# Two early input quads loaded in pairs, and one division moved ahead of a normalization, in a transformer block on one NeuronCore

## The chip, the cores and the metric

The kernel runs on one core of a Trainium2 chip. The metric is device time in microseconds. Three runs of the kernel before took 2637.81 us in the median (2637.12 to 2638.28).

## What is computed

The input x has the shape (2, 256, 128, 128): batch, time, frequency band, channel. Three residual steps follow each other:

```python
xt = _ln(x, ln_t_w, ln_t_b).transpose(0, 2, 1, 3)
x = x + _mha(xt, t_wi, t_bi, t_wo, t_bo, 4, cm).transpose(0, 2, 1, 3)   # causal, over the 256 times
xf = _ln(x, ln_f_w, ln_f_b)
x = x + _mha(xf, f_wi, f_bi, f_wo, f_bo, 4, bm)                         # |i-j| <= 16, over the 128 bands
xn = _ln(x, ln_n_w, ln_n_b)
h = jax.nn.gelu(xn @ w1.T + b1, approximate=False)
x = x + (h @ w2.T + b2)
```

`_ln` is a layer normalization over the 128 channels, `_mha` an attention with 4 heads of 32 channels. All is float32.

## The kernel before, in words

The work is cut into groups of 512 tokens, four tiles of 128. First come all groups of the attention over time (class `OverTime`): 64 per batch, each with two bands at all 256 times. After them come the groups over the bands (`OverBands`) and of the two-layer network (`FeedForward`), in runs of 32 times. The change touches only the first groups over time. They are called by their number here: group 0 to group 3 share one quad of input, `k.x0`; groups 4 to 7 share the second quad, groups 8 to 11 the third, groups 12 to 15 the fourth. A quad is a tile of 128 partitions by 16 by 128 floats, 1 MB, and it is filled by four DMAs of 256 KB, each of which fills 32 partitions. So any group of a quad needs all four of them.

Nothing is reordered by a planner here. Every operation goes through the helper `InOrder` (line 904 of the profile, for that reason) and keeps the order in which the Python code emits it, on its own engine. `start` (line 1197) emits the head, and `run` (line 1261) then runs a loop over n. In the round n of that loop the engines do, interleaved: the second half of the scores of group n and the first half of those of group n+1 on TensorE (`time_scores`, line 754); the exponentials on ScalarE; the masks and a sum on GpSimd; the output product of group n-2 (`output`, `finish`) and the sums and products with the values of group n-1 (`weigh`); the reciprocal by two functions of ScalarE and the division on VectorE for group n-1 (`invert`, `divide`, lines 602 and 615); and the queries, keys and values of group n+2 (`queries_keys`, `values`).

A group's path to TensorE has these steps. `load` (line 382) issues its part of the quad on SyncE's queue. `statistics` (line 390) is four BATCH_NORM_STATS2 and four BATCH_NORM_AGGREGATE on VectorE. Then the inverse root, by GpSimd (`root`) or for several groups together by ScalarE with a refinement on VectorE (`Four`, `root_in_bank`, `refine`, line 429). `normalize` (line 441) is four TENSOR_SCALAR on VectorE into `xh`; `turn` (line 458) is a 32x32 block transpose on VectorE into `z` and four DMAs into a DRAM tile, `turned`; `fetch` (line 470) is one DMA from it into `xnT`. SyncE's queue issues all of these DMAs in their order in the program, and an issue that has to wait holds up all behind it. The first four groups are transposed by TensorE instead (`turn_by_tensor`, line 483), and then copied from PSUM by VectorE.

`divide` works on the PSUM banks of the sums and the weighted values: a product into the bank, `u`, then `oT`. These two banks are taken again by the scores of the next round, so TensorE's scores wait for `u` and `oT`.

The head also loads weights: `rows` (three bias rows, each broadcast to 128 partitions), `w1T` (256 KB) and others. `add_rows` (line 1110) needs the first two rows and `fold_hidden` (line 1180) needs `w1T`, both in round 0. In the kernel before, round 0 emits the four loads of the third quad early in its text and two of the fourth quad's later, round 1 the other two; a round's place in the program is no time, and SyncE issues them as soon as its queue comes to them.

Of the kernel before, what the change touches and what calls it, by code (L numbers as in the profile page):

```python
# [25 lines left out]
NT = 4  # L26
# [7 lines left out]
HALF = P // 2  # L34
# [8 lines left out]
def load_constants(ctx, tc, x, t_wiT, t_woT, f_wiT, f_woT, w1T, w2T, cols, rows):  # L43
    nc = tc.nc
    B, T, FB, C = x.shape
    k = Consts()
    k.NI = w1T.shape[1] // P
    const = ctx.enter_context(tc.tile_pool(name="const", bufs=1))
    k.const = const
    sync, scalar = InOrder(tc, nc.sync), InOrder(tc, nc.scalar)  # L50
    k.x0 = const.tile([P, NT, NT, C], F32, name="x0")

    def tokens(g, n, queues):
        for i in range(NT):
            f = i // (T // P) * NT + g
            queues[i % 2].dma_start(k.x0[rows_of(i), :, g : g + n], BoundedPath.of_times(x[0], i, slice(f, f + n)))

    def weight(src, n, name, queue=sync):
        t = const.tile([P, n], F32, name=name)
        queue.dma_start(t, src)  # L60
        return t

    def rows_in(a, b):
        for i in range(a, b):
            sync.dma_start(k.rows[:, i, :], rows[i : i + 1, :].partition_broadcast(P).squeeze(1))

    def late_weights():
        k.w2T = const.tile([P, k.NI, C], F32, name="w2T_sb")
        sync.dma_start(k.w2T, w2T.rearrange("(j p) c -> p j c", p=P))

    tokens(0, 1, (sync, scalar))
    k.cols = const.tile([P, 16], F32, name="cols_sb")
    sync.dma_start(k.cols, cols)
    k.wiT = [weight(t_wiT, 3 * C, "t_wiT_sb", scalar)]
    scalar.preload_act_table_set(EXP_SET)
    tokens(1, 1, (sync, sync))
    tokens(2, 2, (sync, sync))
    k.woT = [weight(t_woT, C, "t_woT_sb")]
    k.rows = const.tile([P, 3, C], F32, name="rows_sb")
    rows_in(0, 2)  # L80
    k.wiT.append(weight(f_wiT, 3 * C, "f_wiT_sb"))
    k.woT.append(weight(f_woT, C, "f_woT_sb"))
    k.load_w1T = lambda: setattr(k, "w1T", weight(w1T, k.NI * P, "w1T_sb"))
    k.late_weights, k.late_rows = late_weights, lambda: rows_in(2, 3)
    k.ones = const.tile([P, P], F32, name="ones")
    nc.vector.memset(k.ones, 1.0)
    k.ident = const.tile([P, P], F32, name="ident")
    make_identity(nc, k.ident)
    k.mhalf = const.tile([P, NT], F32, name="mhalf")
    nc.vector.memset(k.mhalf, -0.5)  # L90
    dram = ctx.enter_context(tc.tile_pool(name="dram", bufs=1, space=DRAM))
    k.x1 = [dram.tile([T, FB, C], F32, name=f"x1_{b}") for b in range(B)]
    return k
# [548 lines left out]
def rows_of(h):  # L642
    return slice(h * D, (h + 1) * D)
# [265 lines left out]
class BoundedPath:  # L909
# [71 lines left out]
    def groups(self, x, out):  # L981
        nc, k = self.nc, self.k
        B, T, FB, C = x.shape
        NC_T = T // P
        for b in range(B):
            for f0 in range(0, FB, GA):
                held = {}


                def load(g, f0=f0, b=b, held=held):  # L990
                    if b == f0 == 0:
                        held["x"] = k.x0
                        return
                    if g == 0:
                        self.input_quad(held)
                        if b == 0 and f0 == 2 * NT:
                            self.vector.memset(held["x"][:, 0, 0, 0:1], 0.0)
                    f = f0 + g // NC_T * NT
                    self.sync.dma_start(held["x"][rows_of(g)], self.of_times(x[b], g, slice(f, f + NT)))

                def store(g, f0=f0, b=b, held=held):
                    for i in range(NT if g % 2 else 0):
                        f = f0 + i // NC_T * NT + g
                        self.sync.dma_start(
                            self.of_times(k.x1[b], i, slice(f - 1, f + 1)), held["res"][rows_of(i), :, g - 1 : g + 1]
                        )

                def part(name, g, i=None, a=0, held=held):
                    if name == "res" and name not in held:
                        self.quad(held, "res", 2)  # L1010
                    if i is not None:
                        return self.longer(held[name], i * NT + g, a)
                    return held[name][:, :, g]

                for g in range(NT):
                    yield OverTime(self, partial(part, "x", g), partial(part, "res", g), partial(load, g), partial(store, g))
        for b in range(B):
            for r0 in range(0, T, RUN):
                run = []
                for t0 in range(r0, r0 + RUN, GB):  # L1020
                    held = {}
# [21 lines left out]
                    def part(name, g, i=None, a=0, held=held):  # L1043
# [4 lines left out]
                        return held[name][:, g]  # L1048

                    run += [(g, part, load, store) for g in range(NT)]  # L1050
                for g, part, load, _ in run:
                    yield OverBands(self, partial(part, "x", g), partial(part, "x2", g), partial(load, g))
# [144 lines left out]
    def start(self, groups):  # L1197

        first, second, third, fourth, fifth = groups[:5]
        b = self.banks  # L1200
        for group in groups[: 2 * NT]:
            group.load()
        self.k.load_w1T()
        self.warm((0, 1, 5, 2))
        first.statistics()
        self.fold(0, self.vector)
# [27 lines left out]
        second.turn_by_tensor(b["b0"], self.vector)  # L1234
        self.fold_products(1, self.ps[7])
        self.fold_bias(1)
        Attention.place = dict(qp=b["b3"], kp=b["b1"], vp0=b["b0"], vp1=b["b2"])
        first.first_weights(first.early)
        first.first_weights(first.late)
# [21 lines left out]
    def run(self, x, out):  # L1261
        groups = list(self.groups(x, out))

        def do(n, *names):
            if 0 <= n < len(groups):
                for name in names:
                    getattr(groups[n], name)()

        def at(n, kind):
            return 0 <= n < len(groups) and isinstance(groups[n], kind)  # L1270

        def do_at(n, kind, *names):
            if at(n, kind):
                do(n, *names)
# [6 lines left out]
        run0 = [i for i in range(len(groups)) if at(i, OverBands)][: RUN // NT]  # L1281
        times = range(3 * NT, run0[-1] + 1)
        fours = {i + NT - 1: Four(self, groups[i : i + NT]) for i in times[::NT]}
        threes = [Four(self, groups[i : i + 3]) for i in (5, 8)]
        A, k = RUN // NT, self.k
        early = [i for i in range(3, len(groups)) if at(i, FeedForward) and at(i - 3, OverBands)]

        def statistics_of_feed(n):
            if n + 5 in early:
                do(n + 5, "statistics")  # L1290
            if at(n + 4, FeedForward) and n + 4 not in early:
                do(n + 4, "statistics", "root")
# [6 lines left out]
        for n in range(len(groups) + 2):  # L1299
            feeds = [at(n - 2 + i, FeedForward) for i in range(5)]  # L1300
            bands = [at(n - 2 + i, OverBands) for i in range(5)]
            turn = feeds[2] and bands[1]
# [5 lines left out]
            do(n, "first_half", "first_function", "first_mask")  # L1308
            if n == 0:
                do(3, "normalize_flat")  # L1310
            if 1 < n < 5:
                do(n + 7, "statistics")
            if n + 2 * NT in times:
                do(n + 2 * NT, "statistics")
            if old is not None or new is not None:
                time_scores(old, new)
                b = self.banks
# [3 lines left out]
            if old is not None:  # L1321
                old.second_weights(old.late)
                if n + 2 < TURNED:
                    groups[n + 2].turn_by_tensor(b["b0"], self.vector)
                if n == 0:
                    for group in groups[2 * NT : 3 * NT]:
                        group.load()
                    do(5, "statistics")
                    self.fold_output(self.ps[b["b3"]])
                    self.fold_hidden(b["b3"])  # L1330
                    self.add_rows()
                if n == run0[0] - 1:
                    self.square_queries()
                do(n - 2, "output")
# [7 lines left out]
            if new is not None:  # L1342
                new.first_weights(new.early[1:])
            if n == 1:
                threes[0].root_in_spare()
                threes[0].refine()
            if n == 3:
                threes[1].root_in_bank()
            if n == 5:
                do(11, "root_in_bank")  # L1350
            if n + 2 * NT in fours:
                fours[n + 2 * NT].root_in_bank()
            if n == run0[0] - 1:
                self.take_squares()
            if turn:
                do(n, "second_half", "second_function")
            if n + 3 >= TURNED:
                do_at(n + 3, OverTime, "fetch")
            do_at(n + 2, (OverBands, FeedForward), "fetch")
# [2 lines left out]
                k.late_rows()  # L1362
            if n == 5:
                k.late_weights()
            for i in (2 * n + 12, 2 * n + 13) if n < 2 else (n + 14,):
                do(i, "load")
            do_at(n + 3, (OverBands, FeedForward), "normalize", "turn")
            do_at(n + 4, OverTime, "normalize", "turn")
            if old is not None:
                do(n - 2, "finish")  # L1370
            if n == 0:
                do(6, "statistics")
                do(7, "statistics")
            if n == 1:
                do(8, "statistics")
            if n == 3:
                threes[1].refine()
            if n == 5:
                do(11, "refine")
            if n + 2 * NT in fours:  # L1380
                fours[n + 2 * NT].refine()
            if not bands[2] and not turn:
# [7 lines left out]
            if n == len(groups):  # L1390
                self.bounded = self.nc.values_load(self.flag[0:1, 0:1], min_val=0, max_val=1)
            do(n - 1, "divide")
            if bands[2] or turn:
                statistics_of_feed(n)
            if not turn:
# [99 lines left out]
```

## Time and profile before

| | |
|---|---|
| median of three runs | 2637.81 us |
| the profiled execution's own time | 2640.7 us |
| its span, first to last instruction | 2638.7 us |
| TensorE (PE) busy | 2622.6 us, 99% |
| VectorE (DVE) busy | 2141.0 us, 81% |
| GpSimd (POOL) busy | 1955.8 us, 74% |
| ScalarE (ACT) busy | 1838.1 us, 70% |
| SyncE's DMA queue | 50.1% of 16 engines |

The profiled execution is 2.0 us longer than its span and 2.9 us longer than the median of the runs. PE is the engine, PEld its weight loads; a float32 matmul of the program appears twice in the counts. Starts are in us from the first instruction. "issue" is idle time for which the profile shows no semaphore; a releaser in brackets is what ended an idle stretch. DMA issues on SyncE are SPq; a landing time is from issue to completion.

### The profile page before, as it was taken

To read this page: it belongs to the slowest core of one execution; us is meant where nothing else is said; L and a number is where in the kernel's file an instruction comes from. 1 tells how busy PE (TensorE), PEld (TensorE's weight loads), DVE (VectorE), ACT (ScalarE), POOL (GpSimd) and SP (SyncE) were. 2 spreads that over 40 slices of the span, in tenths; PEclk is the share of its full clock that TensorE was granted. 3 is DMA by queue.
4 is the path that set the end of the run, shared out by engine and by line. 5 is a ranking of instruction groups with operands and counts; after the bars stand their busy time and mean duration, and the time that the engine had idled before them with its cause. 6 is when DMAs were issued, how large, how long until landed. Compare 5 with 4: busy or idle time off the path is not lost.

```text
span 2638.7 us, 156452 instructions
## 1 busy us (share of the span) xinstructions
PE 2622.6 (99%) x68688; PEld 1862.4 (71%) x68688; DVE 2141.0 (81%) x6408; ACT 1838.1 (70%) x3543; POOL 1955.8 (74%) x2311
## 2 busy tenths in 40 slices
PE   9999999999999999999999999999999999999998
PEld 6666766667676666777776677777777766777667
DVE  7888888888888887977878779778797797887974
ACT  6899899999989874664655746647557466475573
POOL 7999999999999986666667666665676666657762
PEclk9999999999999999999999999999999999999999
DMA  6665555555656544454444545454544545544543
GB/s 150 156 155 151 150 152 152 153 154 148 156 150 153 126 125 113 123 128 122 119 123 123 124 121 124 123 128 115 126 123 113 128 114 130 128 118 121 122 102 88
DMA packets 469845, 344.97 MB, mean 131 GB/s; under 512 B 43168, under 2 KB 404512, under 8 KB 469152
## 3 DMA queue, kind: packets, MB, share of 16 engines
q1 hardware_dynamic: 468432, 334.41, 50.1%
q8 instruction: 540, 8.85, 1.5%
q14 instruction: 153, 1.25, 0.2%
q10 hardware_dynamic: 720, 0.46, 0.1%
HBM read 167.98 MB, written 166.72 MB: 127 GB/s over the span
## 4 chain that ended last, share of the span: by engine, by line
PE 98%; DVE 1%; POOL 0%; issue 0%; ACT 0%; DMA 0%; ACTq 0%; DVEq 0%; POOLq 0%
PE bank L904 98%; POOL rstd L904 0%; DVE stats L904 0%; DVE xh L904 0%; DMA x<-in_x 0%; DVE ln L904 0%; ACT hT L904 0%; DMA xnT<-turned 0%; ACT p L904 0%; DVE z L904 0%; DVE u L904 0%; POOL res L904 0%; POOL x L904 0%; DVE mv L904 0%; DVE res L904 0%
## 5 line engine op out<-in xcount | busy, mean ns | idle before, releaser
L904 ACT ACTIVATE hT<-bank,b 128x512 f32<-128x512 f32 x512 | 347.6, 688 | 516.3 <-PE bank L904 472.6
L904 POOL TENSOR_SCALAR_AFFINE_SELECT pf<-pf 128x512 f32<-128x512 f32 x768 | 476.7, 635 | 185.0 <-ACT pf L904 158.7
L904 PEld LDWEIGHTS bank<-w2T_sb,hT 128*32 128x32 f32 x16384 | 472.2, 110 | 51.5 <-issue 24.0
L904 PE MATMUL bank<-xnT,wf 128*32 128x512 f32 x4096 | 492.2, 592 | 0.5 <-DVE xnT L904 0.5
L904 PE MATMUL bank<-xnT,w1f 128*32 128x512 f32 x4096 | 491.5, 592 | 0.0
L904 PE MATMUL bank<-w2T_sb,hT 128*32 128x128 f32 x16384 | 487.5, 273 | 1.1 <-issue 0.6
L904 ACT ACTIVATE p<-bank 128x512 f32<-128x512 f32 (+1 forms) x1024 | 430.9, 494 | 67.1 <-PE bank L904 67.1
L904 DVE TENSOR_SCALAR xh<-x,mv,rstd 128x160 f32<-128x160 f32 (+1 forms) x1016 | 395.9, 432 | 59.5 <-POOL rstd L904 49.3
L904 POOL TENSOR_SCALAR_AFFINE_SELECT p<-p 128x1024 f32<-128x1024 f32 (+2 forms) x384 | 363.5, 947 | 62.4 <-ACT p L904 54.1
L904 PEld LDWEIGHTS bank<-wf,xnT 128*32 128x32 f32 x8192 | 243.3, 110 | 144.2 <-issue 97.7
L904 DVE BATCH_NORM_STATS2 stats<-x 128x6 f32<-128x128 f32 x1536 | 329.0, 277 | 3.8 <-DMA x<-in_x 3.8
L904 POOL TENSOR_TENSOR p<-p,p 128x512 f32<-128x512 f32 x256 | 324.0, 1287 | 10.7
L904 POOL TENSOR_SCALAR rstd<-mv 128x4 f32<-128x4 f32 x251 | 57.3, 228 | 363.1 <-DVE mv L904 361.4
L904 PEld LDWEIGHTS bank<-xnT,w1f 128*32 128x32 f32 x4096 | 200.6, 110 | 158.9 <-issue 89.9
L904 PE MATMUL bank<-qT,kT 32*64 32x80 f32 (+4 forms) x16384 | 304.6, 272 | 3.6 <-issue 2.3
L904 PEld LDWEIGHTS bank<-qT,kT 32*64 32x64 f32 x16384 | 261.4, 131 | 55.8 <-ACT kT L904 50.6
L904 DVE TENSOR_TENSOR res<-bank,res 128x512 f32<-128x512 f32 (+1 forms) x259 | 170.5, 658 | 155.4 <-PE bank L904 150.5
L904 ACT ACTIVATE pf<-bank 128x512 f32<-128x512 f32 x512 | 265.6, 602 | 38.4 <-PE bank L904 37.4
L904 PE MATMUL bank<-wn,oT 128*32 128x128 f32 x8192 | 287.5, 275 | 0.6 <-issue 0.4
L904 DVE STREAM_TRANSPOSE z<-xh 128x512 f32<-128x512 f32 x380 | 270.5, 712 | 13.3
L904 PE MATMUL bank<-wf,xnT 128*32 128x128 f32 x8192 | 276.4, 273 | 0.0
L904 POOL TENSOR_TENSOR rstd<-rstd,mhalf 128x4 f32<-128x4 f32 x251 | 260.6, 1038 | 20.9
(101 smaller groups left out, 3828.6 us busy)
## 6 DMA issues: line engine op xcount, KB each, us to landing
turned<-z SPq DMA_DIRECT2D x1520, 64.0 KB, 2.7
xnT<-turned SPq DMA_DIRECT2D x380, 256.0 KB, 3.1
x<-res SPq DMA_DIRECT2D x256, 128.0 KB, 2.6
x<-x SPq DMA_DIRECT2D x128, 256.0 KB, 4.1
out<-res SPq DMA_DIRECT2D x252, 128.0 KB, 2.4
x<-in_x SPq DMA_DIRECT2D x124, 256.0 KB, 4.3
x<-in_x SPq DMA_DIRECT2D x4, 128.0 KB, 2.8
x<-in_x SPq DMA_DIRECT2D x6, 64.0 KB, 2.9
```

The source lines that it names most:

```text
L904: return self.tc.keep_in_program_order(emit(*args, **kwargs))
```

## The change

- The loads of the first two `rows` and of `w1T` are emitted later, after the fold of the second bias in the head, behind a memset of one column of `rows` on VectorE.
- The third quad's loads are emitted in two pairs, in round 0 and round 1, each behind a memset on VectorE that follows the copy of a turned tile from PSUM. The fourth quad's come in two pairs in round 2, the next quad's first two in round 3.
- The memset of the second quad at the start is gone.
- In round 1, `normalize` and `turn` of group 5 come after the division of group 0. The statistics of group 8 move from round 1 to round 2, those of groups 9, 10 and 11 from rounds 2, 3 and 4 to rounds 3, 4 and 5.
- The inverse roots are grouped as (5, 6, 7), (8, 9), (10, 11) instead of (5, 6, 7), (8, 9, 10), (11).

```diff
     k.rows = const.tile([P, 3, C], F32, name="rows_sb")
-    rows_in(0, 2)
...
+    k.early_rows = lambda: rows_in(0, 2)
...
-                    if g == 0:
+                    if "x" not in held:
                         self.input_quad(held)
-                        if b == 0 and f0 == 2 * NT:
-                            self.vector.memset(held["x"][:, 0, 0, 0:1], 0.0)
...
-        self.k.load_w1T()
         self.warm((0, 1, 5, 2))
...
         self.fold_bias(1)
+        self.vector.memset(self.k.rows[:, 0, 0:1], 0.0)
+        self.k.early_rows()
+        self.k.load_w1T()
...
-        threes = [Four(self, groups[i : i + 3]) for i in (5, 8)]
+        sets = [Four(self, groups[i:j]) for i, j in ((5, 8), (8, 10), (10, 12))]
...
-            if 1 < n < 5:
-                do(n + 7, "statistics")
+            if 2 < n < 6:
+                do(n + 6, "statistics")
...
                     groups[n + 2].turn_by_tensor(b["b0"], self.vector)
+                if n < 2:
+                    self.vector.memset(groups[2 * NT].src()[n * HALF :, 0, 0:1], 0.0)
+                    do(2 * NT + 2 * n, "load")
+                    do(2 * NT + 2 * n + 1, "load")
                 if n == 0:
-                    for group in groups[2 * NT : 3 * NT]:
-                        group.load()
...
+            if n == 2:
+                do(12, "load")
+                do(13, "load")
...
-            for i in (2 * n + 12, 2 * n + 13) if n < 2 else (n + 14,):
+            for i in {0: (), 1: (), 2: (14, 15), 3: (16, 17)}.get(n, (n + 14,)):
                 do(i, "load")
             do_at(n + 3, (OverBands, FeedForward), "normalize", "turn")
-            do_at(n + 4, OverTime, "normalize", "turn")
+            if n != 1:
+                do_at(n + 4, OverTime, "normalize", "turn")
...
-            if n == 1:
-                do(8, "statistics")
-            if n == 3:
-                threes[1].refine()
-            if n == 5:
-                do(11, "refine")
+            if n in (3, 5):
+                sets[n // 2].refine()
...
             do(n - 1, "divide")
+            if n == 1:
+                do(5, "normalize", "turn")
+            if n == 2:
+                do(8, "statistics")
```

More of the change, by code (lines that the diff above doesn't have):

```diff
@@ L1010, in part @@
                         self.quad(held, "res", 2)
+                    if name == "x" and name not in held:
+                        self.input_quad(held)
                     if i is not None:
@@ L1344, in run @@
             if n == 1:
-                threes[0].root_in_spare()
-                threes[0].refine()
-            if n == 3:
-                threes[1].root_in_bank()
-            if n == 5:
-                do(11, "root_in_bank")
+                sets[0].root_in_spare()
+                sets[0].refine()
+            if n in (3, 5):
+                sets[n // 2].root_in_bank()
             if n + 2 * NT in fours:
@@ L1373, in run @@
                 do(7, "statistics")
-            if n == 1:
-                do(8, "statistics")
-            if n == 3:
-                threes[1].refine()
-            if n == 5:
-                do(11, "refine")
+            if n in (3, 5):
+                sets[n // 2].refine()
             if n + 2 * NT in fours:
```

## The prediction

> **What bounds the kernel now.** I read the page's busy times first, then who TensorE waited for, then the timeline of the first 60 us with the granted clock in stretches, and last SyncE's queue. Busy times, then TensorE's waits over the whole span:
>
> ```profile
> span 2638.7 us, 156452 instructions
> PE 2622.6 (99%) x68688; PEld 1862.4 (71%) x68688; DVE 2141.0 (81%) x6408; ACT 1838.1 (70%) x3543; POOL 1955.8 (74%) x2311
> PE bank L904 <- issue: 3.5, 8, 2.0
> PE bank L904 <- POOL ident masks.py:199: 1.5, 1, 1.5
> PE bank L904 <- DVE u L904: 1.2, 1, 1.2
> PE bank L904 <- DVE xh L904: 1.2, 1, 1.2
> ```
>
> TensorE is idle for 16.1 us in all (2638.7 - 2622.6), so no change of order can win more than that, apart from clock. About 7 us of it are the stores after the last matmul (2631.65 in the chain of waits), 2.7 us the very start (`ident`, `xh`). What a change in the first rounds can reach are two stalls, one of 2.0 and one of 1.2 us. The timeline there:
>
> ```profile
> 18.20 1.36 PE L904 MATMUL bank<-qT,kT 32*64 32x64 f32 x59
> 21.52 0.33 PE L904 MATMUL bank<-qT,kT 32*64 32x128 f32 x5 [1.96 <-issue]
> ...
> 31.16 1.61 DVE L904 TENSOR_SCALAR xh<-x,mvs,rstds 128x160 f32<-128x160 f32 x4
> 32.81 0.71 DVE L904 STREAM_TRANSPOSE z<-xh 128x512 f32<-128x512 f32 x1
> 33.44 0.83 DVE L904 BATCH_NORM_STATS2 stats<-x 128x6 f32<-128x128 f32 x4
> 34.47 0.67 DVE L904 TENSOR_TENSOR bank<-bank,r 128x512 f32<-128x512 f32 x1
> 35.18 0.69 DVE L904 SCALAR_TENSOR_TENSOR u<-bank,r 128x512 f32<-128x512 f32 x1
> 35.97 0.69 DVE L904 TENSOR_TENSOR oT<-bank,u 128x512 f32<-128x512 f32 x1
> 36.01 2.52 PE L904 MATMUL bank<-qT,kT 32*64 32x256 f32 x50 [1.22 <-DVE u L904]
> ```
>
> Stall 1: with 5 score matmuls to go, TensorE stops at 19.55, and no semaphore ends it. Stall 2: `r` is ready at 31.70 (31.07 + 0.63), but VectorE first normalizes and turns group 5 and takes statistics, and begins the division at 34.47; the scores need its bank. The clock after stall 2, and DMA around stall 1 (columns: length, busy of PE, PEld, DVE, ACT, POOL, then clock, DMA share, GB/s):
>
> ```profile
> 20.00:21.00 1.00, 0.00 (x0) 0.00 (x0) 0.58 (x3) 0.46 (x1) 0.98 (x1) 1.00 1.10 227
> 37.00:38.00 1.00, 1.00 (x36) 1.00 (x20) 1.00 (x9) 0.00 (x0) 0.00 (x0) 0.50 0.27 76
> q8 instruction: 1, 0.02, 8.3%
> ```
>
> The last line is the DMA view of 18 to 19 us: one packet of TensorE's instructions (q8 carries 8.85 MB over the run, about 64 bytes for each of its 137,376 matmuls and loads), the first after the start, beside a queue busy at over 100%. All other engines idle before 21.5, so I take stall 1 for TensorE out of instructions, behind six 256 KB loads:
>
> ```profile
> 10.56 0.43 SPq L904 DMA_DIRECT2D w1T_sb<-in_w1T  x1
> 11.03 5.37 SPq L904 DMA_DIRECT2D x<-in_x  x6
> 27.48 2.90 SPq L904 DMA_DIRECT2D turned<-z  x4
> ```
>
> These land 8.7 to 10.0 us after issue; loads at 32 us and later take 3.9 to 4.5.
>
> **What the Trainium skill says.** "Runtime: NRT & Kernel Launch", Instruction fetch mechanics: instructions are refilled in 16 KiB blocks of 256 by a DMA, mostly hidden. The trace agrees on the size (8.85 MB in 540 packets) and shows one that isn't hidden. "DMA: Bandwidth & Descriptors", Queues, rings and completion order: each DMA engine takes turns between the queues it has work for. That alone wouldn't delay a fetch by long; the trace shows 2 us of stall, so the measurement decides. "TensorE: Matmul & The Clock Gate", Part 1: after an idle window of about 3.4 us, free-running, the clock halves. The trace has 0.50 from 36.9 to 40.3, one such length, after only 1.22 us idle among small score matmuls; after stall 1 it has none.
>
> **Part 1, loads held back.** The six loads leave 11 to 17 us. The first two (a pair of the third quad) now wait for a VectorE memset of 0.06 us (that of `x` took 59 ns) after the copy of group 2's turned tile. `rows` and `w1T` wait for one after bq, at about 15.6. The DMA queue is then drained of the second quad at about 15.5: its loads are issued 8.74 to 10.5 and land 4.9 to 6.9 later even with the rest queued behind. The fetch then starts 2 to 3 us earlier, and lasts as before 3.0 us to the resumption (18.5 to 21.5) or less: ready at 18.5 to 19.5, needed at 19.55. Stall 1 goes: -2.0. Queued behind the memset's wait on SyncE are only `rows` and `w1T`: issued 15.7 to 17.1, with some 3 us to land (`rows` 3.4, `w1T` 7.9 in the crowd) at 20; `fold_hidden` needs `w1T` at 23.12 - 1.97 = 21.15. Slack 1. If the cover is gone, its delay counts one to one.
>
> **Part 2, division first.** With everything 1.97 earlier, `r` is ready at 29.73; VectorE has by then finished the copy for group 3 and the refinement (from 21.08 busy without a break, as from 23.05 before: copy at 27.5 to 28.15, refinement to 29.2). The division runs 29.77 to 31.9. TensorE reaches the scores that need `u` at 34.8 - 1.97 = 32.8. Stall 2 goes. Its size by rounds: queries of groups 3 and 4 start at 31.43 and 42.41, 10.98 apart, those of 4 and 5 at 42.41 and 49.48, 7.07. So the round loses 3.9 us: up to the resumption 1.5 (34.48 to 36.01, with the matmuls' drain), and 2.4 at half clock after it.
>
> **Part 3, what is late next.** Three covers:
> - *xnT of group 5.* Its z now comes at 31.9 + 1.63 + 0.7 = 34.25 (33.5 before, for a need at 49.48). Four issues (1.75) to 36.1; the loads of groups 12 and 13 go out behind them; turned lands 2.9 to 4.1 after the last issue, 39.0 to 40; the fetch then lands 2.9 to 4 later behind 512 KB: 42 to 44. Needed at 31.43 - 1.97 + 2 x 7.07 = 43.6. Cost 0, up to 0.5.
> - *xnT of group 4.* The second pair of the third quad (28.3) goes ahead of its fetch; that lands at about 35, needed 36.5. Nothing.
> - *VectorE.* A round has xh and z 2.26, statistics 1.03, division 2.14, `res` 0.65: 6.1 of 7.07 (start to start). Round 4 has a second statistics (7.1), and so, newly, has round 5, since groups 9 to 11 moved one round down; rounds 3 and 5 also a refinement (0.6): round 5 has 7.7. Adding these from 31.9 on, the division begins 0.6 to 0.7 after `r` in rounds 3 and 4, and 1.2 in round 5, where TensorE has slack for 0.6. So waits of 0.1, 0.1 and 0.6, 0.8 in sum, partly shared with a late xnT. Bounds 0 and 2.
>
> The root of groups 8 and 9 needs no new time (three small operations for three). The memsets cost 0.12 of VectorE, inside that sum; the dropped one was idle time. The second quad's removed memset ended at 1.1 and held nothing. Loads 12 to 17 need to land two rounds before use: 46 against 48 for group 12.
>
> **The sum.** Against the profiled execution: 2638.7 - 2.0 - 3.9 + 0.8 = 2633.6 of span, 2635.6 with the 2.0 around it. The runs' median is 2.9 below that execution's 2640.7. The clock's stretch depends on where a free window falls; three runs within 1.2 us of each other, all below the profiled one, speak for runs without it. So I count it in full for the profile and hardly for the median: 2637.8 - 2.0 - 1.5 + 0.8 = 2635.1; with the clock in full 2632.7. I take 2634.6, a little clock included. That is -0.12%. I call 0.2% (5.3 us) the least that a measurement of this kernel can tell from no change.
>
> **Rivals.**
> - *All of it arrives* (0.25): half-clock stretch in the runs too, covers hold: 2637.8 - 5.9 + 0.3 = 2632.2. For it: the round lost 3.9 in the profile. Against: the runs' closeness.
> - *Given back* (0.2): the fetch still stalls for part (`rows` and `w1T` land in its way), or xnT of group 5 is 1 us late, or VectorE's lag is 2: 2637.8 - 3.5 + 2.5 = 2636.8. For it: slacks of 0 to 1 us above. This is also where the change doesn't do what it says: were stall 1 no fetch, it would stay, 2636.5.
> - *Slower* (0.05): VectorE's lag in rounds 3 to 5 makes a stall of over 1.2 us in each, and each is followed, as at 36.9, by a half-clock stretch of 2.4: 3 x 3.9 = 11.7 against 3.5 gained, 2646. It turns slower once two of three stalls pull the clock down and the third is over 0.7 us. Against: lag 0.7 to 1.2 with 0.6 slack.
>
> **How the numbers follow.** My forecast, stalls gone and under a microsecond back, 0.5: 2633 to 2636. With the rivals, 8 in 10 lie between 2631.8 and 2637.4. Faster by over 0.2% needs under 2632.5: most of the second case, 0.25. Slower by that, over 2643.1, is the last, 0.04. The rest, 0.71, is within.
>
> **What would show it.** Right: no PE wait of 1.96 at 19.5 with DMA share far below 1 at 18 to 22; the division of group 0 ahead of xh at 30, no "DVE u" wait, clock 1.00 throughout; queries of group 4 at about 36.5, 5.9 earlier; VectorE full from 21 to 62. Wrong: a wait on `xnT<-turned` near 43.6, on `oT` or `u` near 47 or 61, or an issue stall still at 19.5. If the runs gain 5 or more, the clock was in them.

## The result, and the profile after

| | before | changed |
|---|---|---|
| median of 22 runs each | 2638.20 us | 2633.32 us |
| ratio (95% interval) | | 0.9981 (0.9975 to 0.9988) |
| span of the profiled execution | 2638.7 us | 2631.4 us |

The change gains 4.9 us in the runs, 0.19%, which lies just within the 0.2% that the prediction called the least that can be told; the interval excludes no change. The forecast was 2634.6, a gain of 3.2 on the median known then. In the two profiled executions the gain is larger, 7.3. The page after, and TensorE's waits over its whole span:

```profile
span 2631.4 us, 156457 instructions
PE 2618.3 (100%) x68688; PEld 1862.3 (71%) x68688; DVE 2140.6 (81%) x6410; ACT 1837.9 (70%) x3543; POOL 1956.4 (74%) x2311
```

```profile
PE bank L904 <- issue: 1.6, 6, 0.4
PE bank L904 <- POOL ident masks.py:199: 1.5, 1, 1.5
PE bank L904 <- DVE xh L904: 1.5, 1, 1.5
PE bank L904 <- DVE xnT L904: 0.5, 1, 0.5
PE bank L904 <- ACT hT L904: 0.3, 2, 0.2
```

The issue wait's longest is 0.4 instead of 2.0, and the wait on `u` is gone. Of what remains at the start, `ident` is as before and `xh` is 1.5 instead of 1.2. The timeline at the two places:

```profile
17.70 1.39 PE L904 MATMUL bank<-qT,kT 32*64 32x64 f32 x64
19.02 1.16 PE L904 MATMUL bank<-ident,xh 128*128 128x128 f32 x8
...
28.97 0.70 DVE L904 TENSOR_TENSOR bank<-bank,r 128x512 f32<-128x512 f32 x1 [0.61 <-ACT r L904]
29.70 0.69 DVE L904 SCALAR_TENSOR_TENSOR u<-bank,r 128x512 f32<-128x512 f32 x1
30.50 0.69 DVE L904 TENSOR_TENSOR oT<-bank,u 128x512 f32<-128x512 f32 x1
31.11 1.60 DVE L904 TENSOR_SCALAR xh<-x,mvs,rstds 128x160 f32<-128x160 f32 x4
31.36 1.39 PE L904 MATMUL bank<-qT,kT 32*64 32x64 f32 x64
```

All 64 score passes run through at 17.7, where 59 and then 5 stood. The division starts as soon as `r` is there, and the scores at 31.36 pass without a break. The first packet of TensorE's instructions after the start is now in the DMA view of 13 to 14 us, beside a queue that is a third full:

```profile
q1 hardware_dynamic: 50, 0.08, 36.7%
q8 instruction: 1, 0.02, 8.2%
```

**Where the time went, by rounds.** A good ruler is the start of each group's queries on TensorE (the first matmul from `xnT`). Distances in us:

| groups | 0 to 1 | 1 to 2 | 2 to 3 | 3 to 4 | 4 to 5 | 5 to 6 | 6 to 7 | 7 to 8 | 0 to 13 |
|---|---|---|---|---|---|---|---|---|---|
| before | 5.79 | 8.63 | 7.32 | 10.98 | 7.07 | 7.08 | 7.08 | 7.08 | 96.43 |
| changed | 5.78 | 6.37 | 7.32 | 7.08 | 7.21 | 7.10 | 7.08 | 7.51 | 90.86 |

Stall 1 was worth 2.26, the round of stall 2 3.90, and 0.14 + 0.02 + 0.43 = 0.59 is given back in later rounds. Of the 7.3 of the spans, 0.5 more stems from the first rounds' start (group 0's queries at 9.19, at 9.69 before; the first loads land 0.3 to 0.5 sooner, though nothing ahead of them was changed), and 1.2 comes after group 13. In all profiled executions group 0's queries begin anywhere between 8.65 and 9.8, and from group 13's queries to the last matmul the two kernels take 2523.4 to 2525.4 in five executions, in no order of kernels. So I count neither as the change's.

The 0.59 is in two places. Busy time of each engine from queries to queries, for groups 4 to 5, 5 to 6 and 7 to 8 (columns: length, PE, PEld, DVE, ACT, POOL, clock, DMA share, GB/s):

```profile
35.74:42.95 7.21, 7.21 (x201) 4.86 (x194) 7.00 (x26) 6.48 (x17) 6.68 (x7) 1.00 1.00 218
42.95:50.05 7.10, 7.10 (x196) 5.03 (x196) 6.82 (x28) 6.44 (x15) 6.38 (x7) 1.00 0.47 130
57.13:64.64 7.51, 7.51 (x200) 5.09 (x196) 6.99 (x22) 6.50 (x15) 6.57 (x7) 1.00 0.52 140
```

In the first, the DMA queue is full (share 1.00, the last figure but one). SyncE's queue, with the fetch of group 5 behind a pair of loads and another pair behind it:

```profile
35.30 0.94 SPq L904 DMA_DIRECT2D x<-in_x  x2
36.75 1.16 SPq L904 DMA_DIRECT2D xnT<-turned  x1
37.96 0.90 SPq L904 DMA_DIRECT2D x<-in_x  x2
```

That fetch lands 6.1 us after its issue, at 42.85; TensorE could have begun at 42.82 and begins at 42.95. In the round from 57.13 it is VectorE:

```profile
57.05 0.63 ACT L904 ACTIVATE r<-ln 128x512 f32<-128x512 f32 x1
58.30 0.70 DVE L904 TENSOR_TENSOR bank<-bank,r 128x512 f32<-128x512 f32 x1
59.03 0.69 DVE L904 SCALAR_TENSOR_TENSOR u<-bank,r 128x512 f32<-128x512 f32 x1
59.83 0.69 DVE L904 TENSOR_TENSOR oT<-bank,u 128x512 f32<-128x512 f32 x1
59.84 1.81 PE L904 MATMUL bank<-qT,kT 32*64 32x64 f32 x64
60.58 0.86 PEld L904 LDWEIGHTS bank<-qT,kT 32*64 32x64 f32 x36 [0.16 <-DVE oT L904]
```

`r` was ready at 57.68 (57.05 + 0.63), the division begins at 58.30, `oT` ends at 60.52, and the scores take 1.81 instead of 1.39: 28 loads of weights go ahead, and the 36 left start at 60.58. The ends of matmuls are modelled, so the busy time hides this wait, and the list of PE's waits doesn't have it.

### The profile page after: what moved, and what is told of

Same layout as the page of the kernel before. It is cut to its first block, busy times and chain, and to the rows that moved or that the text cites. A ratio compares the mean times of both kernels' runs of the same rounds, so it can differ in the third digit from the quotient of the medians.

```text
span 2631.4 us, 156457 instructions
## 1 busy us (share of the span) xinstructions
PE 2618.3 (100%) x68688; PEld 1862.3 (71%) x68688; DVE 2140.6 (81%) x6410; ACT 1837.9 (70%) x3543; POOL 1956.4 (74%) x2311
## 3 DMA queue, kind: packets, MB, share of 16 engines
q14 instruction: 153, 1.25, 0.2%
## 4 chain that ended last, share of the span: by engine, by line
PE 98%; DVE 1%; ACT 0%; issue 0%; DMA 0%; POOL 0%; ACTq 0%; DVEq 0%; POOLq 0%
PE bank L904 98%; DVE xh L904 0%; DVE stats L904 0%; DVE ln L904 0%; ACT hT L904 0%; DMA x<-in_x 0%; DVE z L904 0%; POOL rstd L904 0%; DVE mv L904 0%; DVE x L904 0%; DVE res L904 0%; DVE bank L904 0%; DVE u L904 0%; DVE gs L904 0%; DVE oT L904 0%
## 5 line engine op out<-in xcount | busy, mean ns | idle before, releaser
L904 PE MATMUL bank<-xnT,w1f 128*32 128x512 f32 x4096 | 497.0, 592 | 0.0
```

The lines of the kernel that those rows point to most:

```text
L904: return self.tc.keep_in_program_order(emit(*args, **kwargs))
```

## Experiments

My theory after the result: stall 1 is an instruction fetch that queues behind the early loads; stall 2 is VectorE's order alone; the two are separate; the 0.59 is a late fetch and VectorE. The rivals: the stalls hang together, or other engines make them. One name in the expectations is wrong: what they call "groups 2 to 3" is the distance from group 1 to group 2. Times are medians beside the kernel before on the same chip. The ratio and its interval are not the quotient of these two medians: here they differ from it by up to 0.0009, or 2.4 us, so a single gain below is known no better than about that. The distances are from one profiled execution of each.

### Division first, alone

Edit, against the kernel before:

```diff
-            do_at(n + 4, OverTime, "normalize", "turn")
+            if n != 1:
+                do_at(n + 4, OverTime, "normalize", "turn")
...
             do(n - 1, "divide")
+            if n == 1:
+                do(5, "normalize", "turn")
```

> The kernel before with only the normalization and turn of group 5 moved behind the first division. Theory (two separate causes: stall 1 is an instruction fetch queued behind the early loads, stall 2 is VectorE's order): queries of groups 2 to 3 stay 8.6 us apart, with the issue stall of about 2 us; groups 3 to 4 come down from 10.98 to 7.1, no wait on u, no half-clock stretch; time 1.5 us under before if the half clock is rare in the runs, 3.9 if it is common. Rival (stall 2 only follows from the late loads): groups 3 to 4 stay near 11.

Measured: 2636.42 against 2637.94, ratio 0.9993 (0.9987 to 1.0000). Groups 1 to 2: 8.08; 3 to 4: 7.09; 4 to 5: 8.25. TensorE's lines of stall 1, and then what is new:

```profile
21.09 0.33 PE L904 MATMUL bank<-qT,kT 32*64 32x128 f32 x5 [1.41 <-issue]
```

```profile
39.44 0.65 DVE L904 TENSOR_TENSOR res<-bank,res 128x512 f32<-128x512 f32 x1
40.14 0.81 PEld L904 LDWEIGHTS bank<-wf,xnT 128*32 128x32 f32 x32 [1.06 <-DVE res L904]
```

The theory holds for the two stalls. But the next round gives 1.2 back: group 5's normalization and turn now stand in front of the next round's work on VectorE, where the statistics of groups 8 and 9 still are, and `res` comes late for the values of group 4: it begins 8.4 us after group 3's queries, in the changed kernel 7.0. So, by the two traces, the moved statistics, which I had counted as a cost alone, make the room for the division's move. The time doesn't tell the two forecast sizes apart: 1.5 us by the medians, 0 to 3.4 by the interval, with 1.2 given back.

### Loads held, the division where it was

Edit, against the changed kernel:

```diff
-            if n != 1:
-                do_at(n + 4, OverTime, "normalize", "turn")
+            do_at(n + 4, OverTime, "normalize", "turn")
...
-            if n == 1:
-                do(5, "normalize", "turn")
```

> The changed kernel with the normalization and turn of group 5 back ahead of the first division. Theory: groups 2 to 3 come to 6.4 as in the changed kernel, groups 3 to 4 go back to 8.6 (stall of 1.2 on u) or to 11 if the clock halves after it; time 2.3 to 2.8 under before. Rival (stall 2 goes with the loads): groups 3 to 4 at 7.1 and the changed kernel's whole gain of 4.9.

Measured: 2635.39 against 2637.94, ratio 0.9986 (0.9979 to 0.9993). Groups 1 to 2: 6.37, as forecast. Groups 3 to 4: 8.33, less than the 8.6:

```profile
32.11 1.78 PE L904 MATMUL bank<-qT,kT 32*64 32x256 f32 x50 [0.20 <-DVE u L904]
32.81 0.86 PEld L904 LDWEIGHTS bank<-qT,kT 32*64 32x64 f32 x36 [0.17 <-DVE oT L904]
33.82 1.08 PE L904 MATMUL bank<-wn,oT 128*32 128x128 f32 x32
```

```profile
51.59 0.42 PE L904 MATMUL bank<-p,v 128*32 128x128 f32 x8 [0.51 <-issue]
57.60 0.95 PE L904 MATMUL bank<-wn,oT 128*32 128x128 f32 x25 [1.33 <-issue]
```

The statistics that stood between normalization and division are gone here too, so the wait on `u` falls from 1.22 to 0.20, and no half-clock stretch follows. Yet the round still loses 1.25 (8.33 - 7.08) at full clock, because `oT` holds the scores too: 36 of the 50 loads of weights start only when it is done, and the 50 passes take 1.71 (32.11 to 33.82), longer than the 1.32 of all 64 in the changed kernel. The division begins 0.68 before the scores here, and 0.34 after them in the kernel before, 1.02 later. So stall 2 costs about 1.25 + 1.02 = 2.3 at full clock, an estimate from the two traces, and not the 1.2 that the list of waits shows.

Later rounds lose more than expected (7.87, 8.62, 7.42, 7.92 up to group 12), two of them by issue stalls. In this one profile 0 to 13 is 95.53, hardly less than before; the runs gained 2.5 us by the medians and 3.7 by the ratio. By the medians neither move alone comes to the 4.9; the interval here, 1.8 to 5.5 us, would still allow it.

### rows and w1T at their old places

Edit, against the changed kernel:

```diff
+    rows_in(0, 2)
     k.wiT.append(weight(f_wiT, 3 * C, "f_wiT_sb"))
...
+        self.k.load_w1T()
         self.warm((0, 1, 5, 2))
...
-        self.vector.memset(self.k.rows[:, 0, 0:1], 0.0)
-        self.k.early_rows()
-        self.k.load_w1T()
```

> The changed kernel with rows and w1T loaded at their old places, the quads still held. Theory (what matters is the 1.5 MB of the six quad loads): the fetch's packet starts by 14, groups 2 to 3 stay at 6.4, time as the changed kernel. Rival (every byte ahead of the fetch counts): w1T's 256 KB moves the packet to 15 to 16, still without a stall. If groups 2 to 3 go to 7 or more, holding rows and w1T is part of the gain.

Measured: 2634.07 against 2637.94, ratio 0.9978 (0.9972 to 0.9985). The fetch's packet starts at 16.18 instead of 13.0, and groups 1 to 2 are 6.71 apart, 0.34 more: the 64 score passes take 1.66 instead of 1.32. The packet is close to the rival's 15 to 16 and not to mine, though the rival had no stall. So these loads alone bring back more than half of the fetch's delay, but TensorE feels only what comes after its need, and 0.34 is below what the runs can tell: in time, holding `rows` and `w1T` is a small part of the change.

### The quads early again

Edit, against the changed kernel:

```diff
+        for group in groups[2 * NT : 3 * NT + 2]:
+            group.load()
         self.warm((0, 1, 5, 2))
...
-                if n < 2:
-                    self.vector.memset(groups[2 * NT].src()[n * HALF :, 0, 0:1], 0.0)
-                    do(2 * NT + 2 * n, "load")
-                    do(2 * NT + 2 * n + 1, "load")
...
-            if n == 2:
-                do(12, "load")
-                do(13, "load")
```

> The changed kernel with four loads of the third quad and two of the fourth issued in the head again, ahead of the held rows and w1T. Theory: the fetch's packet starts at 18 or later and the issue stall of about 2 us is back, groups 2 to 3 at 8.6 or more (w1T, now behind the six loads, lands near 25 and may add to it); groups 3 to 4 stay at 7.1, since the division is first. Rival (the loads' place is nothing to the stall): 6.4.

Measured: 2639.96 against 2637.94, ratio 0.9999 (0.9991 to 1.0008); groups 1 to 2 9.71 apart, 3 to 4 7.08; the packet at 17.57.

```profile
17.46 1.36 PE L904 MATMUL bank<-qT,kT 32*64 32x64 f32 x59
20.50 0.33 PE L904 MATMUL bank<-qT,kT 32*64 32x128 f32 x5 [1.68 <-issue]
...
23.46 1.05 PE L904 MATMUL bank<-cols_sb,w1T_sb 128*128 128x1 f32 x8 [1.09 <-DMA w1T_sb<-in_w1T]
```

TensorE stops after the same 59 passes, with 5 to go, and `w1T` behind the loads adds 1.09. With these six loads in the head, the gain is gone. That is the strongest evidence for the first step. Two numbers tie the stall to the packet. In all five profiled executions that have it (the kernel before three times, the division alone, and this one) TensorE stops after the same 449 recorded matmuls and weight loads; and while the packet starts anywhere between 17.51 and 18.97, TensorE resumes 2.93 to 3.04 us after it.

### Unneeded copies in their place

Edit, against the changed kernel, with six copies; for three it has `range(3)`:

```diff
+    k.spare = dram.tile([6, P, NT, C], F32, name="spare")
+    k.spare_from = lambda i: x[1, 0:P, NT * i : NT * (i + 1), :]
...
+        for i in range(6):
+            self.sync.dma_start(self.k.spare[i], self.k.spare_from(i))
         self.warm((0, 1, 5, 2))
```

> The changed kernel with six copies of 256 KB from HBM to HBM, whose data nobody reads, issued where the kernel before issued its six early loads. Theory (the fetch waits behind whatever is queued): packet at 18 or later, an issue stall of 2 us or more on TensorE, groups 2 to 3 at 8.6 or more; rows and w1T come behind the copies too, so w1T can add to it. Rival (the loads took TensorE's time through their own data or buffers): 6.4, no stall.

> The same with three such copies, half the bytes. Theory: the packet starts between, about 15.5 to 16.5, and is usable 3 us later at 18.5 to 19.5, just in time: stall 0 to 0.5. Rival (a threshold on how many transfers are outstanding, not bytes): as with six, or nothing at all with the packet at 13.

Measured with six: 2637.12 against 2639.56, ratio 0.9991 (0.9982 to 1.0000), groups 1 to 2 7.55 apart. With three (a profile alone): 6.41. The packets start at 15.14 and 14.93, not at 18 and 15.5 to 16.5. For six, 15 to 16 us in the DMA view, and TensorE's timeline:

```profile
q1 hardware_dynamic: 210, 0.38, 99.6%
q8 instruction: 1, 0.02, 6.0%
```

```profile
17.16 1.39 PE L906 MATMUL bank<-qT,kT 32*64 32x64 f32 x64
...
21.01 1.05 PE L906 MATMUL bank<-cols_sb,w1T_sb 128*128 128x1 f32 x8 [0.92 <-DMA w1T_sb<-in_w1T]
```

A miss. The queue is as full (99.6%) as it was in the kernel before (104.5%), but the fetch is only 2.1 us later than in the changed kernel, so it is in time, and three copies delay it as much as six. What is lost is the wait for `w1T`. So neither the bytes queued nor a full queue set the fetch's delay by themselves. Loads into SBUF delay it more than copies of the same size within HBM, and why is open. One rival was not tested: the copies pass faster. At a share of about 1 they move 377 to 397 GB/s from 14 to 17 us, while the loads of the kernel before move 195 to 262 from 12 to 18, so six copies fill the queue for less time than six loads do; but the packet starts some 3 us before they are through.

### Statistics of group 13 a round later

Edit, against the changed kernel:

```diff
-            if n + 2 * NT in times:
+            if n + 2 * NT in times and n != 5:
                 do(n + 2 * NT, "statistics")
+            if n == 6:
+                do(13, "statistics")
```

> The changed kernel with the statistics of group 13 one round later, so round 5 has one statistics. Theory (round 5 is VectorE's: 7.7 us of work in a 7.08 us round): groups 7 to 8, 7.51 apart in the changed kernel, come down to 7.1; groups 4 to 5 stay at 7.2. Rival (w2T's load or ScalarE makes the 0.43): 7.5 stays.

> The changed kernel with the statistics of group 13 in round 6, timed. Theory: 0.4 us under the changed kernel, which is less than these runs can tell; groups 7 to 8 at 7.1 again. Not better than that, since no other wait is touched.

Measured: groups 7 to 8 7.08 apart, in both profiles (4 to 5: 7.11 and 7.08). The 0.43 was VectorE's. The second profile loses 0.39 elsewhere, with groups 5 to 6 at 7.47. Timed: 2634.66, beside 2634.99 for the changed kernel on the same chip (ratios to before 0.9979, 0.9970 to 0.9989, and 0.9980, 0.9974 to 0.9987): no difference that the runs can tell.

### Loads of groups 12 and 13 behind the fetch

Edit, against the changed kernel:

```diff
-            if n == 2:
-                do(12, "load")
-                do(13, "load")
...
-            for i in {0: (), 1: (), 2: (14, 15), 3: (16, 17)}.get(n, (n + 14,)):
+            for i in {0: (), 1: (), 2: (12, 13, 14, 15), 3: (16, 17)}.get(n, (n + 14,)):
```

> The changed kernel with the loads of groups 12 and 13 behind the fetch of group 5 instead of ahead of it. Theory (the fetch waits behind 512 KB on the way): the fetch lands in 3 to 4 us instead of 6.1, groups 4 to 5 at 7.08 instead of 7.21; the 0.43 in round 5 stays. Rival (VectorE makes the 0.13 too): 7.2 stays.

Measured: groups 4 to 5 7.08 apart, as forecast. But 5 to 6 9.24, 2.16 more, which no theory had:

```profile
46.12 1.47 PE L904 MATMUL bank<-qT,kT 32*64 32x64 f32 x55 [0.55 <-issue]
...
50.82 0.43 PE L904 MATMUL bank<-p,v 128*32 128x128 f32 x8 [0.29 <-issue]
51.67 1.92 PE L904 MATMUL bank<-xnT,wf 128*32 128x512 f32 x15 [0.42 <-DMA xnT<-turned]
```

Four loads in one go, 1 MB, stand ahead of the turned copies of group 6, which take 6.3 us to land instead of 5.0, and so delay its fetch. The next instruction packet starts at 43.44, in the changed kernel at 42.46, so it may be held up too. The 0.43 of groups 7 to 8 falls to 0.06, since TensorE is later. In this one profile, loads in pairs with a transfer between them are the better trade; the variant has no other run.

### Both kernels again

> The kernel before, looked at again. Theory: the 2.0 issue stall and the stall on u come in every execution (groups 2 to 3 about 8.6, groups 3 to 4 at 8.6 or more), since queue and order are fixed; the half-clock stretch depends on the phase of a free window, so groups 3 to 4 are 8.6 without it and 11 with it. If it is there each time, its 2.4 us belong to the gain of the runs too.

> As the look before: stalls the same, the half clock perhaps.

> The changed kernel, looked at again on the chip of the next run. Theory: rounds as in its first profile, 6.4 for groups 2 to 3, 7.1 for 3 to 4, 7.1 to 7.2 for 4 to 5, 7.5 for 7 to 8; ratio to before 0.998.

The kernel before: groups 1 to 2 9.25 and 9.45 apart, 3 to 4 10.99 and 11.00. In stretches of one us, the second profile and then the third (columns as above; the clock is the third figure from the end):

```profile
22.00:23.00 1.00, 1.00 (x7) 1.00 (x7) 1.00 (x4) 0.94 (x2) 0.94 (x2) 0.50 0.87 172
39.00:40.00 1.00, 1.00 (x32) 1.00 (x34) 1.00 (x9) 0.00 (x0) 0.00 (x0) 0.53 0.10 20
```

```profile
38.00:39.00 1.00, 1.00 (x23) 0.56 (x16) 1.00 (x7) 0.29 (x2) 0.00 (x0) 0.50 0.00 0
```

The half-clock stretch after stall 2 is there in all three profiled executions, each time with the round at 11. In the second there is another after stall 1 as well, and groups 2 to 3 take 9.71 instead of 7.32. These two stretches begin at 22.00 and 39.06, five times 3.41 us apart, and they last two such lengths and one: they lie on one grid of 3.41 us. At the end of each of the three executions, after the last matmul, the clock falls once more, 761 such lengths after the stretch that follows stall 2; so the grid holds through an execution, and it stands elsewhere in each. The changed kernel's second profile: 6.37, 7.08, 7.17 and no such stretch while matmuls run, but groups 6 to 7 at 8.05, by a fetch that is 0.8 late, and then 7 to 8 at 7.10, not the 7.5 expected:

```profile
57.87 1.50 PE L904 MATMUL bank<-xnT,wf 128*32 128x512 f32 x12 [0.77 <-DMA xnT<-turned]
```

So what is given back differs from one execution to the next: 0 to 13 is 90.86 and 91.72, against 96.43, 99.83 and 97.27 before.

## Why the prediction was right, and where it was off

- **Bounds and ceiling.** Right: what could be won was the two stalls and the clock after the second.
- **Part 1.** Right, 2.0 forecast and 2.26 measured; the fetch moved by 5.5 us (18.5 to 13.0), more than the 2 to 3 forecast. Putting the loads back puts the stall back. How the loads delay the fetch is less clear than I wrote: copies in the same place, with the queue as full, don't delay it as much.
- **Part 2.** Right that stall 2 goes, and the round shortens by 3.90. This size was read from the profile before, so its return doesn't test how the 3.9 divides, and there the prediction was wrong (see the mis-sized term). VectorE's work was not without a break, as it said: it waits 0.46 for ScalarE at 30.1, which changed nothing. That the move costs nothing on VectorE held only because the statistics were moved too; alone it gives 1.2 back.
- **Part 3.** Right in kind and nearly in size. The late `xnT` of group 5: 42 to 44 forecast for a need of 43.6, landed at 42.85 for 42.82, cost 0.1. VectorE: 0.1, 0.1, 0.6 forecast for the divisions of rounds 3, 4 and 5, which the distances 5 to 6, 6 to 7 and 7 to 8 show: 0.02, 0.00 and 0.43, and moving one group's statistics removed the last. Here two errors met, so the closeness is partly luck: in round 5 the division begins 0.62 after `r` and not 1.2, but 0.62 with a slack of 0.6 should have cost nothing, so the slack was nearer 0.2. The 0.14 of groups 4 to 5 is mostly the fetch. `w1T` was in time (20.46, no wait).
- **The sum.** Span 2633.6 forecast, 2631.4 measured; of the 2.2 between, 0.2 is the smaller give-back and 0.3 the larger stall 1, the rest lies outside the rounds that the change touches.
- **The term that was mis-sized** is the clock: "I count it in full for the profile and hardly for the median". Its size was wrong first. The 3.9 was divided into 1.5 for the stall and 2.4 at half clock; but 3.41 us at half clock cost 1.7 at most, and the other 2.2 are the stall itself, waits on `u` and `oT` together, as the second experiment shows at full clock (2.3). Without any clock the forecast should have been 2634.4, not 2635.1.
- **Its share in the runs** was wrong too. The record has the mean granted clock of each run, to 0.001, which is worth 2.6 us. It counts a last stretch at half clock, after the last matmul, that every profiled execution of both kernels has and that costs TensorE nothing. Beside the first four experiments the kernel before has 0.998 or less in 31 of 67 runs, and the two variants that hold the quads' loads (the second and the third experiment) in none of 42. Beside the last runs it is 15 of 30 against 2 of 21 for the changed kernel; the means are 0.9984 and 0.9992, a difference worth about 2.2 us (an estimate, from rounded figures) of the 5.1 between the medians. So the clock belongs to the runs of the kernel before, on average by somewhat more than one stretch of 1.7, though not to every run: 4 of the 67 have 1.000. In which round it fell in the timed runs isn't on record; the first experiment, where only stall 1 is left, still has 0.998 in 5 of 22.
- **The total.** Counting the round's 3.9 in full, with stall 1 at 2.3 and 0.6 given back, makes 2638.2 - 2.3 - 3.9 + 0.6 = 2632.6, closer to 2633.3 than 2634.6 was, and nearer to the rival called "all of it arrives" (2632.2) than I allowed. The closeness of three runs was no argument: 22 runs of the same kernel spread from 2636.0 to 2642.4.
- **Open.** Over groups 0 to 13 the profiled executions gain between 4.7 and 9.0, with means of 97.8 before and 91.3 after, 6.6 apart; the medians of the runs gain 4.9 and 5.1. Three and two executions are too few to call this a difference: the one with the long stretch after stall 1 makes 1.0 of it. Whether the recording of a profile adds to the stalls of the kernel before wasn't tried.

## What to carry to other kernels

A prefetch that nobody needs yet isn't free: it can stand ahead of the next instructions and of transfers that are needed, and holding it behind a wait on an earlier result cost nearly nothing here (a memset of 0.06 us on VectorE for each hold). When a chain on a nearly full engine is reordered, ask what the moved work will now stand in front of, and make room there in the same edit. Measure a stall by the length of its round and not by the list of waits, and price it with the half-clock stretch that can follow it, separately.

## What the runs showed that I had not expected

- Stall 2, 1.2 us in the list of waits, together with small score matmuls, was followed by 3.4 us at half clock in each of three executions at different times (36.9, 37.8, 39.1), while stalls of 1.4 to 2.8 us at 20 us were followed by one in only one of five executions (6.8 us long).
- Much of the spread of the runs goes with the clock: the kernel before took 2635.7, 2637.4, 2640.6 and 2643.4 us in the mean of its runs with a mean clock of 1.000, 0.999, 0.998 and 0.997 (4, 32, 22 and 9 runs of the 67).
- An instruction packet that starts at 13.0 to 13.6 us with the loads held started at 15.1 behind six copies of 256 KB within HBM, and at 17.5 to 19.0 behind six loads of 256 KB into SBUF.
- A wait of 0.43 us on VectorE shows only in a round's length (7.51 instead of 7.08) and in a weight load's release, not in TensorE's own list of waits.
